# A Soft-MoE macaron kernel on one core: transposes moved from TensorE to VectorE, products packed into row and column groups of the array, loads ordered by use

## The chip, the cores and the metric

The kernel runs on one core of a Trainium2 chip. TensorE (PE) multiplies matrices, its weight loads (PEld) overlap its products, and its results land in PSUM; VectorE (DVE) and ScalarE (ACT) read PSUM, GpSimd (POOL) works on SBUF alone, and SyncE (SP) issues most DMAs. Each engine works through its own queue in order. The metric is the device time of one execution in microseconds. All data is fp32, and each fp32 product of the program appears in the trace as two PE instructions, each with a weight load, while a transpose appears as one.

## The reference

The input `x` has 8 batches of 256 tokens of 128 features. Six blocks are added to it, each on a layernorm of `x`: Soft-MoE (halved), linear attention, Soft-MoE (halved), a ternary GLU (halved), FAVOR+ attention, and the GLU again (halved). Cut to what the change touches:

```python
# Soft-MoE: 16 experts of 64 slots, hidden size 256
x = layernorm(x) * norm_g + norm_b
se = (layernorm(slot_embeds) * slot_g + slot_b) * scale
logits = einsum('bnd,esd->bnes', x, se)
dispatch = softmax(logits, axis=1)               # over the tokens
combine = softmax(logits.reshape(b, n, -1), -1)  # over all 1024 slots
slots = einsum('bnd,bnes->besd', x, dispatch)
gate = gelu(einsum('besd,edf->besf', slots, Wg) + bg)
up = einsum('besd,edf->besf', slots, Wu) + bu
eout = einsum('besf,efo->beso', gate * up, Wd) + bd
out = einsum('bns,bso->bno', combine, eout)

# FAVOR+: 16 heads of 8, 32 random features each
xw = einsum('bhtd,hmd->bhtm', q, proj); xw -= max(xw, -1)
phi = exp(xw) * exp(-0.5 * sum(q * q, -1)) + 1e-6   # for q and for k
KV = einsum('bhtm,bhtd->bhmd', phi_k, v); Ksum = sum(phi_k, over t)
out = einsum('bhtm,bhmd->bhtd', phi_q, KV) / (phi_q . Ksum + 1e-6)
```

## The kernel before

The work is written as small steps: a step names the engines that can do it with a cost on each, the cells that it reads and writes, and a function that issues its instructions. `Plan.place` puts the steps one by one on an engine where they can start first by those costs, and ties are settled by a key; the list `SHIFTS` moves the keys of parts of the program, and its numbers were found by a search. `Plan.issue` then issues every step in the order of its planned start, so the order in each queue is fixed when the program is built. Buffers (`Buf`) come from pools of fixed slots: "comb" (128x2048), "k4" (128x1024), "k2", "k1", "we" (an expert's weights), "ps" (the 8 PSUM banks) and so on.

The 8 batches form two groups of four, the second planned behind the first, so that work of both is mixed. `group` runs, for each of two MoE layers, `dispatch` on its four batches, `experts`, and `combine` with `linear` (linear attention, first layer only); then `glu` on pairs of batches, `favor` on each batch, and `glu` again with the store of `x`.

`dispatch(b)` normalizes a batch (statistics on DVE, L386 and L387; the root on POOL, L392 and L393; the scaling on either, L399), transposes it on PE (L356, the helper of every PE transpose) and forms the logits: 8 products of 128 slots by 256 tokens (L537), copied out to `comb` by L363 (ACT) or L365 (DVE), with a running maximum on DVE (L554). For each half of the slots, DVE takes the maximum over the tokens (L569), ACT the exponentials with their sums (L577), POOL multiplies by the inverse (L590), and since the next product sums over tokens, eight blocks of 128x128 are transposed on PE (L356) and copied out, and L611 gathers the slots with two products of 512 columns. ACT or DVE scales the result into `slots` (L441, L443). For the combine weights, the maximum over the slots is folded (L631), transposed, reduced (L642), spread over the partitions with a product against the identity (L651), subtracted on POOL (L663), and ACT takes the exponential (L669).

`experts` fetches the weights of each of the 16 experts (L688, L689 on SP), forms gate and up for the four batches at once (L703: 256 columns), applies gelu on ACT (L709) and the product on DVE (L714), and forms the down product for two batches at a time (L733: 128 rows that hold two batches' 64 slots), whose bias DVE adds in two instructions on 64 partitions each (L743). `combine` is L772; the hidden layers of `glu` are L990, its other products L1060, L1063 and L1090.

`favor(b)` squares q and k on POOL, sums the squares of each head with products of 16 columns (`half_norms`, L1154), projects q and k with 32-row products in four row groups of the array (`projected`, L1168, with `tile_position`), subtracts the maximum, takes the exponential, adds 1e-6 to phi(k) on POOL (L1200), sums phi(k) with v in products of 33 columns (`sums`, L1230), masks the blocks of the heads (`blocks`), and multiplies with phi(q) in four column groups (`products`, L1261).

Of the kernel before, what the change touches and what calls it, by code (L numbers as in the profile page):

```python
# [16 lines left out]
    -1227, -613, -401, -68, -58, -18, -64, -450, -1382, -1020, -424, -281, -256, -288, -233,  # L17
    -157, -79, -415, -2474, -2414, -2140, -1616, -1392, -1410, -1361, -1647, -1993, -981, -1024,
    -765, -300, -356, -285, -548, -633, -125, 202, -436, 1069, 1221, 47, 271, -1474, 20, 20,
    328, 135, 321, 41, 324, 244, 344, -354, 285, -285, 130, -858, -387, -2, -20, -1081, -1196,  # L20
    -1025, -690, 2, -62, -155, -432, -31, 11, 73, 364, -325, 423, 704, 1277, 1488, 0, -230,
    -498, -161, 261, 336, -1069, -2039, -294, 15, -985, -97, 217, 334, -2546, -904, 699, 282,
    280, 343, -499, -1613, -348, 575, -245, 854, 1080, -1505, 7, 181, -43, 85, 275, 63, 263,
    275, -549, 207, -31, 105, -21, -515, -1151, -524, -514, -318, -600, -516, -298, -150, -63,
    -195, -1899, -1808, -1825, -1479, -1755, -1468, -2181, -1630, -332, -1392, -135, -1924,
    -2484, -1986, -1337, -312, -863, 129, -9, -422, 292, 66, 420, 268, 35, 18, 226, 263, 558,
    1104, 691, -956, -1572, -901, -704, -964, -1303, -1243, -1820, -2476, -2535, -1146, -830,
    -744, 683, -666, -1356, -722, 275, 396, -1669, -293, -1310, -784, 170, 576, 457, 239, 57,
    785, 684, 309, 781, 1213, 1341, 704, 927, 758, 229, 1188, -1400, 467, 1275, -975, 2, 61,
    -923, 156,  # L30
# [34 lines left out]
class Plan:  # L65
# [7 lines left out]
    LAG = {"PE": 300, "ACT": 120, "DVE": 100, "POOL": 150, "SP": 2200}  # L73
# [128 lines left out]
def macaron_kernel(ctx: ExitStack, tc: tile.TileContext, i: dict, out: bass.AP):  # L202
# [27 lines left out]
        "comb": (NJ * N, 9),  # L230
        "slots": (NJ * NB * 4 * S1, G),
        "k4": (1024, 6),
# [3 lines left out]
        "we": (6 * P + D, 3),  # L236
# [5 lines left out]


    for at, cells in (
        (5000, ["begin"]), (7000, [("x", b) for b in range(B)]), (7500, ["small"]),
        (15000, ["weights"]),
    ):
        plan.given(at, cells)
# [11 lines left out]
    def load(name, shape, src=None, eng=nc.sync):  # L260
        t = const.tile(shape, F32, tag=name, name=name)
        eng.dma_start(t, i[name] if src is None else src)
        return t


    x = const.tile([P, NT, D], F32, tag="x", name="x")
    xin = i["L0_attn_x"].rearrange("b (p t) d -> p b t d", t=TT)
    xout = out.rearrange("b (p t) d -> p b t d", t=TT)

    def x_of(b, n=1):  # L270
        return x[:, b * TT : (b + n) * TT, :].rearrange("p (b t) d -> p b t d", t=TT)

    se_raw = Buf("k4", (P, NJ, D))
    sein = i["slot_embeds"].rearrange("(j p) d -> p j d", p=P)
    for h in range(2):
        part = slice(4 * h, 4 * h + 4)
        step(
            {"SP": 100},
            lambda _, part=part: nc.scalar.dma_start(se_raw.ap[:, part], sein[:, part]),
            ["begin"], [(se_raw, h)],  # L280
        )
    nc.sync.dma_start(x_of(0, 2), xin[:, 0:2])
    sg = load("slot_g", [P, 1], eng=nc.scalar)
    sb = load("slot_b", [P, 1], eng=nc.scalar)
    sc = load("scale", [P, 1], i["scale"].partition_broadcast(P), eng=nc.scalar)
    ng = load("norm_g", [P, 1])
    nb = load("norm_b", [P, 1])
    for q in range(1, 4):
        nc.sync.dma_start(x_of(2 * q, 2), xin[:, 2 * q : 2 * q + 2])
    bg = load("bg", [P, E, 2], eng=nc.gpsimd)  # L290
    bu = load("bu", [P, E, 2], eng=nc.gpsimd)
    wqkv = load("WqkvT", [P, 3 * D])
    wproj = load("WprojT", [P, D])
    bproj = load("bproj", [P, D], i["bproj"].partition_broadcast(P))
    w1 = load("w1T", [P, NH])
    w2w = load("w2T", [P, NH])
    s1 = load("s1", [P, NO])
    s2 = load("s2", [P, NO])
    w3s = load("w3T", [P, NO, D], i["w3T"].rearrange("(k p) o -> p k o", p=P))
    s3 = load("s3", [P, D], i["s3"].partition_broadcast(P))  # L300
    wq = load("WqT", [P, D])
    wk = load("WkT", [P, D])
    wv = load("WvT", [P, D])
    wo = load("WoT", [P, D])
    bo = load("bo", [P, D], i["bo"].partition_broadcast(P))
    proj = load("projT", [P, M])
# [5 lines left out]
    def block_mask(n, value, name):  # L312

        w = P // n
        t = const.tile([P, n], F32, tag=name, name=name)
        nc.gpsimd.memset(t, value)
        nc.gpsimd.affine_select(
            out=t, in_=t, compare_op=ALU.is_ge, fill=0.0, base=0,
            pattern=[[-w, n]], channel_multiplier=1,
        )  # L320
        nc.gpsimd.affine_select(
            out=t, in_=t, compare_op=ALU.is_ge, fill=0.0, base=w - 1,
            pattern=[[w, n]], channel_multiplier=-1,
        )
        return t

    m16 = block_mask(H, 1.0, "m16")
    half16 = block_mask(H, 0.5, "half16")
    m4 = block_mask(4, 1.0, "m4")
# [5 lines left out]
    seT = const.tile([P, NJ, 3, S], F32, tag="seT", name="seT")  # L335
# [37 lines left out]
    def normalized(tiles, twice=False):  # L373
# [15 lines left out]
        def root(_):  # L389
            v = mv.ap[:, 1 : 2 * n : 2]  # L390
            eps = EPS * EPS / (1.0 + EPS) if twice else EPS
            nc.gpsimd.tensor_scalar(v, v, eps, None, ALU.add)  # L392
# [3 lines left out]
        step({"POOL": 600 + 160 * n}, root, [mv], [mv])  # L396
        for t, (dst, src, r, w) in enumerate(tiles):
            def apply(e, t=t, dst=dst, src=src):
                (nc.gpsimd if e == "POOL" else nc.vector).tensor_scalar(  # L399
                    dst(), src(), mv.ap[:, 2 * t : 2 * t + 1], mv.ap[:, 2 * t + 1 : 2 * t + 2],  # L400
                    ALU.subtract, ALU.mult,
                )

            step({"POOL": 840, "DVE": 430}, apply, [r, mv], [w])
# [43 lines left out]
    def keys():  # L448
# [8 lines left out]
        for h in range(2):  # L457
            js = range(4 * h, 4 * h + 4)
# [7 lines left out]
            pse = ps_(4, 2, S)  # L466

            def turn(_, pse=pse, js=js):
                for j in js:
                    flip(pse.ap[:, j % 4].rearrange("p k s -> p (k s)"), se_n.ap[:, j, :])  # L470

            step({"PE": flips(4)}, turn, [(se_n, j) for j in js], [pse])
            part = slice(js[0], js[0] + 4)

            def finish(e, pse=pse, part=part):
                if e == "ACT":
                    nc.scalar.activation(
                        seT[:, part, 0:2], pse.ap, AF.Identity, bias=bs, scale=gs
                    )
                else:  # L480
                    nc.vector.tensor_scalar(
                        seT[:, part, 0:2], pse.ap, gs, bs, ALU.mult, ALU.add
# [3 lines left out]
            step({"ACT": act(512, True), "DVE": dve(512, 120)}, finish, [pse, "gs"], cells)  # L486

            def again(_, part=part):
                nc.gpsimd.tensor_copy(seT[:, part, 2], seT[:, part, 0])

            step({"POOL": 400}, again, cells, [("seT2", j) for j in js])

    def weights():

        def block(_):
            nc.vector.tensor_reduce(
# [15 lines left out]
        step({"DVE": 500}, block, ["weights"], ["pbd"])  # L514
        step({"POOL": 1900}, scaled, ["weights"], ["w3s"])

    def dispatch(b, sl):
# [3 lines left out]
        odd, q = b % 2, b % BG  # L527
        y = norm(b, True)
        yt = transposed(y, TT, True)
        comb = Buf("comb", (P, NJ, N))  # L530
        pm = Buf("k2", (P, 2, N))
        for u in range(4):
            pl = ps_(2, N)

            def logits(_, u=u, pl=pl):
                for j in range(2):
                    mm(  # L537
                        pl.ap[:, j, :],
                        seT[:, 2 * u + j, odd : odd + 2].rearrange("p k s -> p (k s)"),
# [841 lines left out]
```

## Time and profile before

| | |
|---|---|
| median of 3 runs | 777.72 us (777.15 to 778.01) |
| the profiled execution | 777.5 us, of which its span is 775.8 us |
| granted clock of TensorE | 0.999 |
| PE, DVE, ACT, POOL busy | 754.0, 528.2, 450.4, 351.2 us |
| PE instructions | 4584 |
| DMA over the span | 36.96 MB, 48 GB/s |
| first PE instruction, first L703, end of the last PE instruction | 11.31, 54.95, about 772 us |

A group of the profile has a line, an engine, an operation, what it writes from what it reads, the shapes and the number of instructions, then its busy time and the mean duration of one in ns, then the idle time of the engine just before it and what ended that. Matmuls are pipelined, so the mean duration of one (276 ns for 128 columns) is longer than what it adds to a row of them. A line of the timeline has start, length and the number of instructions merged in it.

### The profile page before, as it was taken

What the parts mean: (1) busy time and instruction counts of PE and PEld (TensorE: products, weight loads), DVE (VectorE), ACT (ScalarE), POOL (GpSimd) and SP (SyncE); (2) the same over time, 40 slices, a digit from 0 to 9 for tenths busy, and PEclk for the clock granted to TensorE, in tenths of its full rate; (3) what the DMA queues carried; (4) which work ended last, traced back from release to release, by engine and by line L of the source; (5) the groups of instructions that cost most, each with busy time, mean ns of one, the idle gap of its engine ahead of it and who ended that gap; (6) DMA issues with size and microseconds to landing.
All of it is one profiled execution on the core that took longest, in us unless ns stands there. A gap on an engine that the chain in (4) does not pass through costs nothing.

```text
span 775.8 us, 12408 instructions
## 1 busy us (share of the span) xinstructions
PE 754.0 (97%) x4584; PEld 631.6 (81%) x4584; DVE 528.2 (68%) x1156; ACT 450.4 (58%) x824; POOL 351.2 (45%) x376
## 2 busy tenths in 40 slices
PE   2999999999999999999999999999999999999998
PEld 1768787898888988888889879889777887868787
DVE  4899888668988788885645453566865458885422
ACT  1888999555977689987443332345544327543422
POOL 6969454524618356248932123533721326424210
PEclk9999999999999999999999999999999999999999
DMA  7102323203231123232432200000000000000000
GB/s 195 40 0 64 89 65 118 68 29 116 72 114 34 56 68 96 73 86 76 135 95 67 80 1 1 1 1 1 1 1 1 0 15 1 1 1 1 14 0 28
DMA packets 27579, 36.96 MB, mean 48 GB/s; under 512 B 3808, under 2 KB 18816, under 8 KB 27520
## 3 DMA queue, kind: packets, MB, share of 16 engines
q1 hardware_dynamic: 25968, 35.62, 15.6%
q8 instruction: 36, 0.59, 0.3%
q10 hardware_dynamic: 1488, 0.53, 0.3%
q14 instruction: 23, 0.19, 0.1%
q0 software_dynamic: 64, 0.03, 0.0%
HBM read 35.12 MB, written 1.05 MB: 47 GB/s over the span
## 4 chain that ended last, share of the span: by engine, by line
PE 95%; POOL 1%; DVE 1%; DMA 1%; ACT 0%; SPq 0%; issue 0%; POOLq 0%
PE ps L990 25%; PE ps L703 14%; PE ps L772 7%; PE ps L733 7%; PE ps L611 7%; PE ps L537 7%; PE ps L356 6%; PE ps L1090 4%; PE ps L1060 4%; PE ps L1063 4%; PE ps L1230 2%; PE ps L1168 1%; PE ps L1261 1%; PE ps L820 1%; PE ps L651 1%; PE ps L1154 1%
## 5 line engine op out<-in xcount | busy, mean ns | idle before, releaser
L363 ACT COPY k<-ps 128x512 f32<-128x512 f32 (+1 forms) x99 | 51.6, 533 | 128.2 <-PE ps L990 79.7
L703 PE MATMUL ps<-slots,we 128*128 128x256 f32 x512 | 121.0, 380 | 0.0
L703 PEld LDWEIGHTS ps<-slots,we 128*128 128x128 f32 x512 | 93.8, 189 | 16.6 <-issue 4.3
L990 PE MATMUL ps<-comb,comb 128*128 128x256 f32 x448 | 102.8, 380 | 0.0
L990 PE MATMUL ps<-comb,slots 128*128 128x256 f32 x448 | 101.9, 381 | 0.0
L663 POOL TENSOR_TENSOR comb<-comb,k 128x1024 f32<-128x1024 f32 x32 | 75.1, 2365 | 57.3 <-ACT k L577 29.6
L990 PEld LDWEIGHTS ps<-comb,slots 128*128 128x128 f32 x448 | 83.8, 190 | 13.4 <-issue 1.9
L990 PEld LDWEIGHTS ps<-comb,comb 128*128 128x128 f32 x448 | 83.4, 190 | 11.8 <-issue 1.4
L975 POOL TENSOR_TENSOR comb<-comb 128x512 f32<-128x512 f32 x20 | 30.6, 1530 | 123.9 <-ACT comb L1012 73.3
L590 POOL TENSOR_TENSOR k<-k,sm 128x1024 f32<-128x1024 f32 x32 | 60.6, 1903 | 35.7 <-DVE sm L585 34.3
L356 PE MATMUL ps<-ident,k 128*128 128x128 f32 x408 | 60.1, 276 | 15.1 <-POOL k L399 13.6
L714 DVE SCALAR_TENSOR_TENSOR k<-ps,bu,k 128x256 f32<-128x256 f32 x128 | 57.3, 477 | 22.7 <-ACT k L709 21.7
L709 ACT ACTIVATE k<-ps,bg 128x256 f32<-128x256 f32 x128 | 56.4, 473 | 26.1 <-PE ps L703 25.2
L1004 DVE TENSOR_TENSOR comb<-ps,k 128x512 f32<-128x512 f32 x48 | 33.0, 688 | 55.2 <-PE ps L990 31.9
L356 PEld LDWEIGHTS ps<-ident,k 128*128 128x128 f32 x408 | 49.0, 143 | 26.0 <-POOL k L399 14.6
L733 PEld LDWEIGHTS ps<-we,k 128*128 128x128 f32 x512 | 63.9, 192 | 4.9 <-issue 2.4
L743 DVE TENSOR_TENSOR slots<-ps,we 64x256 f32<-64x256 f32 x128 | 53.8, 421 | 20.3 <-PE ps L733 17.4
L537 PE MATMUL ps<-k,seT 128*128 128x256 f32 x256 | 63.4, 389 | 2.5 <-ACT k L441 1.6
L733 PE MATMUL ps<-we,k 128*128 128x128 f32 x512 | 65.4, 275 | 0.0
L577 ACT ACTIVATE k<-comb,sm 128x256 f32<-128x256 f32 x128 | 63.3, 497 | 1.4 <-DVE sm L569 1.2
L1012 ACT ACTIVATE comb<-comb 128x512 f32<-128x512 f32 x48 | 29.9, 628 | 54.2 <-DVE comb L1004 54.1
L772 PE MATMUL ps<-slots,comb 128*128 128x129 f32 x512 | 60.4, 275 | 0.0
(144 smaller groups left out, 1425.5 us busy)
## 6 DMA issues: line engine op xcount, KB each, us to landing
we<-in_We SPq DMA_DIRECT2D x64, 384.0 KB, 3.1
we<-in_bd SPq DMA_DIRECT2D x64, 64.0 KB, 3.1
x<-in_L_attn_x SPq DMA_DIRECT2D x4, 256.0 KB, 5.8
comb<-in_h2T SPq DMA_DIRECT2D x4, 256.0 KB, 3.3
slots<-in_h1T SPq DMA_DIRECT2D x4, 256.0 KB, 4.9
out<-x SPq DMA_DIRECT2D x8, 128.0 KB, 1.7
k<-in_slot_embeds ACTq DMA_DIRECT2D x2, 256.0 KB, 6.2
k<-in_hs SPq DMA_DIRECT2D x2, 256.0 KB, 4.3
```

What stands on the lines that cost most here:

```text
L356: nc.tensor.transpose(po, src, ident)
L537: mm(pl.ap[:, j, :], seT[:, 2 * u + j, odd : odd + 2].rearrange("p k s -> p (k s)"), yt.ap, start=True, stop=True,)
L577: nc.scalar.activation(ex.ap[:, j, :], comb.ap[:, 4 * h + j, :], AF.Exp, bias=mx.ap[:, j : j + 1], accum_out=mx.ap[:, 4 + j : 5 + j],)
L590: nc.gpsimd.tensor_tensor(ex.ap, ex.ap, mx.ap[:, 8:12].unsqueeze(2).to_broadcast([P, 4, N]), ALU.mult)
L611: mm(po.ap.rearrange("p j k s -> p (j k s)"), y.ap[:, t, :], dm.ap[:, t, :], start=(t == 0), stop=(t == TT - 1),)
L663: nc.gpsimd.tensor_tensor(raw, raw, mb.ap.unsqueeze(1).to_broadcast([P, 4, N]), ALU.subtract)
L703: mm(pe.ap[:, m, :], we.ap[:, ts(2 * m + c, P)], sl.ap[:, j, :, k::2, 0:S], start=True, stop=True,)
L709: nc.scalar.activation(ga.ap, pe.ap[:, 0, :], AF.Gelu, bias=bg[:, e, c : c + 1])
L714: nc.vector.scalar_tensor_tensor(ht.ap[:, c, :], pe.ap[:, 1, :], bu[:, e, c : c + 1], ga.ap, ALU.add, ALU.mult,)
L733: mm(po.ap[:, q, :], ht.ap[:, c, ts(q, P)], we.ap[:, ts(4 + c, P)], start=(c == 0), stop=(c == 1),)
L772: mm(po.ap[:, t, 0 : D + 1], comb.ap[:, j, ts(t, P)], eo()[:, j, q, 0 : D + 1], start=(j == 0), stop=(j == NJ - 1),)
L990: mm(bank.ap[:, o], w(k)[:, c, ts(o, P)], rhs().rearrange("p (c n) -> p c n", c=2)[:, c, :], start=(start and o + c == 0), stop=(stop and ...
```

## The change

In the MoE, POOL's divided exponentials are turned by VectorE in place, in blocks of 32x32 (`nc.vector.transpose`), and no longer by PE. The transposed blocks hold tokens in groups of 32 partitions, so the gather is made of 32-row products in four row groups of the array, each with a PSUM bank of its own. Its other operand, the normalized tokens, must then lie four times over the partitions: SP writes them to DRAM in four DMAs and reads them back in four. The exponentials lie in a "comb" buffer. The down products of two experts share the array, 64 columns each, so that the 128 partitions of the result are the two experts' slots and the bias is added in one instruction; the slots have another layout, an expert's front waits for all slots of the four batches, and the biases of two experts are fetched together. The spread of the token maximum is a transpose.

In FAVOR+, the half norms and the sums of phi(k) are formed in four column groups, with the roles of the operands swapped; a copy and PE transposes turn the results back.

The small constants come in one load, the first inputs are loaded in pieces in the order of their use, all on SP; the weights of the later blocks are loaded after that. PE multiplies the identity by itself 14 times at the start, and ACT takes one exponential. Some scalar instructions of POOL have a second operation (times 1.0) or a changed sign. The pools have other numbers of slots, some costs of the planner are changed, and `SHIFTS` has new numbers.

```diff
 kinds:
-        "comb": (NJ * N, 9),
+        "comb": (NJ * N, 10),
-        "k4": (1024, 6),
+        "k4": (1024, 4),
-        "we": (6 * P + D, 3),
+        "we": (6 * P + D, 4),
...
+    plan.key = -100000
+    x_in(0, 1)
+    keys_in(0)
+    fetched(lambda: small, i["small"], [], ["small", "ng"])
+    keys_in(1)
+    x_in(1, 1)
+    keys_in(2)
+    keys_in(3)
+    for b in range(2, B, 2):
+        x_in(b, 2)
+    plan.key = 0
...
 normalized, root:
-            nc.gpsimd.tensor_scalar(v, v, eps, None, ALU.add)
+            m = mv.ap[:, 0 : 2 * n : 2]
+            nc.gpsimd.tensor_scalar(v, v, 1.0, eps, ALU.mult, ALU.add)
+            nc.gpsimd.tensor_scalar(m, m, -1.0, 0.0, ALU.mult, ALU.add)
             nc.gpsimd.tensor_tensor(v, v, power[:, 0:n], ALU.pow)
 normalized, apply:
-                    ALU.subtract, ALU.mult,
+                    ALU.add, ALU.mult,
...
+    def replicated(y, b):
+        yr = Buf("k4", (P, N // 32, D))
+        def spill(_):
+            for k in range(4):
+                nc.sync.dma_start(
+                    spilled[b].rearrange("i (t k) d -> i k t d", k=4)[:, k],
+                    y.ap[32 * k : 32 * k + 32],
+                )
+        def spread(_):
+            for a in range(4):
+                nc.sync.dma_start(yr.ap[32 * a : 32 * a + 32], spilled[b])
+        step({"SP": 1800}, spill, [(y, t) for t in range(TT)], [("y", b)])
+        step({"SP": 1800}, spread, [("y", b)], [yr])
+        return yr
...
 dispatch:
+        yr = replicated(y, b)
...
-            for t in range(TT):
-                pt = ps_(4, P)
-                def turn(_, t=t, pt=pt, ex=ex):
-                    for j in range(4):
-                        flip(pt.ap[:, j, :], ex.ap[:, j, ts(t, P)])
-                step({"PE": flips(4)}, turn, [ex], [pt], takes=[dm])
-                evacuated(
...
-                    mm(
-                        po.ap.rearrange("p j k s -> p (j k s)"), y.ap[:, t, :], dm.ap[:, t, :],
-                        start=(t == 0), stop=(t == TT - 1),
+            def turn(_, part=part):
+                nc.vector.transpose(
+                    ex.ap[:, part].rearrange("p j n -> p (j n)"),
+                    ex.ap[:, part].rearrange("p j n -> p (j n)"),
+                )
+            step({"DVE": 1200}, turn, [(ex, h)], [(ex, h)])
+        pos = [ps_(NJ, 32) for _ in range(4)]
+        def gathered(_):
+            for c in range(N // 32):
+                for a, po in enumerate(pos):
+                    rows = slice(32 * a, 32 * a + 32)
+                    mm(
+                        po.ap, yr.ap[rows, c, :], ex.ap[rows, :, 32 * c : 32 * c + 32],
+                        start=(c == 0), stop=(c == N // 32 - 1), tile_position=(32 * a, 0),
+                    )
+        for a, po in enumerate(pos):
             affinely(
+                lambda a=a: sl.ap[:, :, a // 2, q, 32 * (a % 2) : 32 * (a % 2) + 32],
+                lambda po=po: po.ap, [po], [(sl, "in", q, a)], NJ * 32,
             )
...
 spread:
-                mm(
-                    pb.ap[:, ts(t, P)], mn.ap[:, t : t + 1].to_broadcast([P, P]), ident,
-                    start=True, stop=True,
-                )
+                flip(pb.ap[:, ts(t, P)], mn.ap[:, t : t + 1].to_broadcast([P, P]))
...
 experts, front:
-                    {"PE": mms(256, 256)}, hidden, [we, *whole(j)], [pe], takes=[ga, (ht, c)]
+                    {"PE": mms(256, 256)}, hidden, [we, *whole(j), *filled], [pe], takes=[ga, (ht, c)]
 experts, back:
+                for q in range(BG):
                     for c in range(2):
-                        mm(
-                            po.ap[:, q, :], ht.ap[:, c, ts(q, P)], we.ap[:, ts(4 + c, P)],
-                            start=(c == 0), stop=(c == 1),
-                        )
+                        for k in range(2):
+                            mm(
+                                po.ap[S * k : S * k + S, q, :], hts[k].ap[:, c, ts(q, S)],
+                                wes[k].ap[:, ts(4 + c, P)], start=(c == 0), stop=(c == 1),
+                                tile_position=(0, S * k),
+                            )
...
+                nc.vector.tensor_tensor(
+                    eo()[:, j, :, 0:D], po.ap,
+                    wes[0].ap[:, 6 * P :].unsqueeze(1).to_broadcast([P, BG, D]), ALU.add,
+                )
...
 favor:
-                    mm(
-                        pn.ap[:, k, t, :], qk.ap[:, 1, k, ts(t, P)], half16,
-                        start=True, stop=True,
-                    )
+                    g = 32 * (k * TT + t)
+                    mm(
+                        ph.ap[g : g + 32, :], half32, qk.ap[:, 1, k, ts(t, P)],
+                        start=True, stop=True, tile_position=(0, g),
+                    )
+        evacuated(lambda: hn.ap, lambda: ph.ap, [ph], [hn], P)
+            lambda _: flip(pn.ap.rearrange("p k t h -> p (k t h)"), hn.ap), [hn], [pn],
...
-                    mm(
-                        pk.ap[:, c, :], phi.ap[:, 1, t, ts(c, P)], v1.ap[:, t, c, :],
-                        start=(t == 0), stop=(t == TT - 1),
-                    )
+                        mm(
+                            pk.ap[32 * c : 32 * c + 32, m, :],
+                            ones32 if m else v1.ap[:, t, ts(c, 32)], phi.ap[:, 1, t, ts(c, P)],
+                            start=(t == 0), stop=(t == TT - 1), tile_position=(0, 32 * c),
+                        )
...
+        step({"DVE": 430}, blocks, [pk], [kvm])
+        step({"PE": flips(2)}, turn_sums, [kvm], [pkt])
+        evacuated(
+            lambda: kv.ap, lambda: pkt.ap.rearrange("p a (c n) -> p a c n", c=4), [pkt], [kv], N
+        )
...
+    def rehearse(_):
+        for _ in range(14):
+            mm(pwarm.ap, ident, ident, start=True, stop=True)
```

## The prediction

> **What bounds the kernel now.** I read the busy table first, then the chain of waits, then the table by stretch, to see whether the bound holds everywhere.
>
> ```profile
> PE 754.0 (97%) x4584; PEld 631.6 (81%) x4584; DVE 528.2 (68%) x1156; ACT 450.4 (58%) x824; POOL 351.2 (45%) x376
> PE 95%; POOL 1%; DVE 1%; DMA 1%; ACT 0%; SPq 0%; issue 0%; POOLq 0%
> ```
>
> TensorE is busy for 754.0 of 775.8 us and is 95% of the chain that ended last. The stretches (columns: length, PE, PEld, DVE, ACT, POOL busy, clock, DMA share, GB/s):
>
> ```profile
> 0.00:10.00 10.00, 0.00 (x0) 0.00 (x0) 1.90 (x12) 0.77 (x1) 3.70 (x20) 1.00 0.62 179
> 10.00:20.00 10.00, 5.47 (x13) 3.46 (x14) 7.68 (x38) 2.44 (x4) 9.30 (x15) 1.00 0.79 216
> 20.00:30.00 10.00, 8.35 (x42) 6.91 (x41) 8.53 (x14) 7.04 (x20) 9.72 (x15) 1.00 0.15 57
> 30.00:40.00 10.00, 10.00 (x55) 7.54 (x54) 8.52 (x16) 9.85 (x33) 9.53 (x7) 1.00 0.01 2
> 60.00:70.00 10.00, 10.00 (x57) 7.88 (x56) 9.03 (x22) 9.84 (x16) 9.23 (x5) 1.00 0.16 46
> ```
>
> From 30 us on PE never starves, but until the experts thin out DVE and ACT run at nine tenths too: PE work taken out there counts only as far as they follow. Before 30 us the inputs and then POOL and DVE hold PE back. So the sum is made in PE time, with the opening apart.
>
> Since matmuls overlap, I price an instruction from runs in the timeline: (run − last one's own duration) / (number − 1). An fp32 product is two PE instructions, a transpose one.
>
> ```profile
> 36.05 1.04 PE L356 MATMUL ps<-ident,k 128*128 128x128 f32 x8
> 761.37 1.95 PE L1090 MATMUL ps<-w3T,comb 128*128 128x128 f32 x16
> 525.82 2.54 PE L990 MATMUL ps<-comb,comb 128*128 128x256 f32 x11
> 528.29 1.17 PE L1168 MATMUL ps<-pbd,k 32*128 32x128 f32 x32
> 529.39 1.99 PE L990 MATMUL ps<-comb,comb 128*128 128x256 f32 x8
> 560.77 1.89 PE L990 MATMUL ps<-comb,slots 128*128 128x256 f32 x8
> 562.60 1.07 PE L1261 MATMUL ps<-k,kv 128*32 128x256 f32 x16
> 563.60 1.07 PE L1154 MATMUL ps<-half,k 128*128 128x16 f32 x8
> ```
>
> Transpose (1.04−0.276)/7 = 0.109 us; 128 columns 0.112; 256 columns 0.216 (and 512: 0.429). Sixteen columns (L1154) cost 0.112 as well. L1168 holds four row groups at once: its 32 instructions take 529.39−528.29 = 1.10, eight groups of four at 0.112 plus 0.20; the L990 run ahead takes 2.47 for 11×0.216 = 2.38. So row-grouped work runs at four for one, and entering and leaving it costs 0.20+0.09 = **0.30 us** a block. L1261 (column groups of 32): 1.00 = 4×0.216+0.14, plus 0.10 ahead: **0.23 us** a block.
>
> **What the Trainium skill says.** "TensorE: Matmul & The Clock Gate", Part 3, has four 32-row tiles measured at 3.07 times one; here 32×0.112 = 3.58 us shrinks to 1.10+0.09 = 1.19, 3.0 times, so it agrees. "TensorEngine Tiling (Array Packing)", Key Properties, says that a change of tiling mode drains TensorE, which is the 0.30 and 0.23 us; it lists two tiles of 128×64, which no run shows yet. Part 1 of the first page says that an idle array runs at half clock: the eight L537 instructions at 16.86 take 3.78 us, about 0.43 each against 0.216 later. For the VectorE transpose "VectorE: DVE Perf Modes", The three transpose paths, gives 32×32 blocks and 311 ns for 128x128 bf16; no trace here has one.
>
> **The change, PE time first.**
>
> ```profile
> L356 PE MATMUL ps<-ident,k 128*128 128x128 f32 x408 | 60.1, 276 | 15.1 <-POOL k L399 13.6
> L611 PE MATMUL ps<-k,k 128*128 128x512 f32 x128 | 59.9, 593 | 0.0
> L651 PE MATMUL ps<-ident,sm 128*128 128x128 f32 x64 | 9.7, 276 | 0.0
> L733 PE MATMUL ps<-we,k 128*128 128x128 f32 x512 | 65.4, 275 | 0.0
> L1230 PE MATMUL ps<-kv,comb 128*128 128x33 f32 x128 | 15.0, 273 | 0.0
> L743 DVE TENSOR_TENSOR slots<-ps,we 64x256 f32<-64x256 f32 x128 | 53.8, 421 | 20.3 <-PE ps L733 17.4
> L569 DVE TENSOR_REDUCE sm<-comb 128x4 f32<-128x1024 f32 x32 | 38.6, 1209 | 0.1
> ```
>
> 1. Dispatch, 16 times. Out: 16 transposes (16×0.109 = 1.74) and eight L611 instructions (8×0.429 = 3.43). In: 32 products of 256 columns in four row groups, 64 instructions in 16 groups of four: 16×0.216+0.30 = 3.76. 1.41 less, **−22.6 us**.
> 2. Token maximum spread by transposing: 64×0.112 → 32×0.109, **−3.7**.
> 3. Expert down products: 512×0.112 = 57.3 becomes 1024 instructions on 64-column halves. If pairs run side by side, 512×0.112 again, plus 32 blocks×0.23: **+7.4**. Bounds: below, no switch cost, 0; above, no overlap, +57.3. I take +7.4, since both group shapes that the trace shows overlap fully.
> 4. FAVOR+, 8 times. Half norms: 8×0.112 → two groups of four, a switch and a transpose, 0.22+0.23+0.11: −0.34. Sums: 16×0.112 → 8×0.112+0.23+2×0.109: −0.45. Together **−6.3**. The new waits (norms → copy → transpose; sums → mask → transpose → copy) stand in PE's queue mostly with other matmuls between, often eight L990 (1.7 us), against 0.4 us copies; what queues behind PE is everything, so I keep +2 for them in the range.
>
> Sum −25.2 us. PE's start-to-start work is 775.8−11.3 (first matmul)−3.7 (after the last) = 760.8. All instructions at the prices above come to 744; the other 16 are gaps, 9 of them before 30 us and 7 later (switches, short stalls). 744 becomes 719.
>
> **The other engines.** DVE: L743's 128×0.42 = 53.8 become 32 of 128x512, at the 0.69 of such PSUM reads (L1004) 22: −32. In come 32 transposes of 128x1024. Bounds: an instruction of 128x1024 [...] as in L569, 1.2 us; twice that if fp32 goes at half rate: +38 to +77. I take 1.2. Copies of the PE transposes (64 of 128x512, by the copies counted in both built programs about 31 fewer on ACT and 33 on DVE) go: −22 and −18; slot copies get smaller and twice as many: ACT +9. DVE ends near 521, ACT near 440, of 755: enough cover on average. Buffers: the exponentials take a "comb" slot now; with both groups' four results held, two of the ten are free for them, so two dispatches at a time can be under way, as few as DVE can feed.
> POOL: half constants and sign changes make two-operand forms; one instruction more per norm (48×0.23 = 11). What the new forms take is not shown: for L1200 between 1.1 (a 512-wide L1132) and the 2.8 measured, for L399 0.48 (DVE's) to 0.82. I count 0: POOL has 55% to spare after the opening.
> SP: eight issues more a dispatch (y to DRAM, four row copies back), 128×0.43 = 55 us of a queue that mostly waits. From y, the copies need 8×0.43 and two landings of about 3 us, 9.5 us. Meanwhile y is transposed, logits (3.5), maximum (1.2), exponentials (2), division (1.9) and transposes (1.2) pass on the other branch: over 10 us, so hidden, with 1 us to spare at worst; if a "we" load ahead of it in SP waits, that margin goes and L644, with all of PE behind it, waits.
> Loads by use: x of batch 0 (128 KB) is alone in front; its first statistic waited for it to 7.96, now to about 4.2 (0.8 issue, 3 to land, as small loads do). All opening loads now go through SP, ten issues at 0.45 to 5.3 us, and leave ACT's queue and POOL's (bg and bu, 1.35 us). The 14 practice products (28×0.21 = 6 us cold) run on an idle PE and save the 1.7 us of half clock, but they may hold the first transposes to about 9.5.
>
> **The opening.** The first expert product (L703) came at 54.95. In the order of the built program all four gathers and their slot copies stand ahead of it now. PE needs by then only 32×0.109+64×0.216+4×3.76 = 32.4 us. DVE has ahead of the last slot copy, each at its duration less the 0.08 us by which neighbours overlap (L554 and L365 start at 25.09, 25.69 and 26.29 and last 0.68): 22 statistics at 0.40, 12 maxima at 0.60, 8 reductions and 8 transposes at 1.12, 16 norms and affines at 0.45, 7 folds and copies at 0.5, 15 small at 0.13: 46 us. Before, DVE was busy 86% of the time from its first data to 54.95; 46/0.88 from 4 us on gives **56 us**. So the faster loads are spent on the transposes, and the opening, not PE, sets that date.
> Span = 56 + (719−32.4) + 7 (gaps later, as before: 16 less the 9 before 30 us) + 3.7 = **753**; 2 us for FAVOR's waits and SP: 755. The profiled execution took 777.5 for a span of 775.8, and the median is 777.72: **757 us**.
>
> **Rivals.**
> A. Openings shrink as the loads do: DVE starts 4 us earlier and POOL's norms halve, first expert at 46: 10 less, 747. For: POOL at 9.3 to 9.7 of 10 there. Against: DVE's 46 us. 0.12.
> B. DVE becomes the bound of the MoE: transposes of 2.4 us put 9.6 us on the opening, and in stretches like 60:70 DVE has one tenth left: 767 to 772. 0.12.
> C. (slower) The two 64-column halves take turns: 57.3 on top, 757+57−7 = **807**. For: no run shows the shape, and twice the weight loads come with it. Against: L1168 and L1261. It decides from 0.152 us a pair (0.112 + the 20.7 us left / 512). 0.07.
> D. (slower or nothing) Late copies through DRAM: PE waits at every gather. From 1.3 us each (16×1.3 = 20.7) the gain is gone; at 2 us it is 757+32 = 789. For: SP's fetches wait up to 45.5 us for a "we" buffer (its waits), and copies queue behind them. Against: the 10 us branch. 0.06, with it that the order searched anew doesn't fill PE, at the same price.
> The forecast as worked: 0.63, with its own range 749 to 766.
>
> **Numbers.** Faster (over 0.2%, 1.6 us, about what runs from 777.15 to 778.01 can tell): 0.63+0.12+0.12 less 0.02 = 0.85; within 0.2%: 0.03; slower: 0.12. Range 744 to 772: the forecast, A and B.
>
> **What would show it.** Right: L644 as 1024 instructions in about 60 us; L356's line down to 272 transposes; L768 near 65 us; DVE transposes at 1.1 to 1.3 us; first expert product at 50 to 60; PE full after that at a busy total near 730. Wrong: L768 over 78 us (C); idle of PE before L644 with a DMA or SP named (D); PE gaps beyond 60 us ended by DVE (B).

## The result, and the profile after

The changed kernel takes **781.44 us** (median of 5 runs, 779.5 to 782.22), the kernel before 777.65 us (5 runs, 777.15 to 778.01). The ratio is 1.0044 with a 95% interval of 1.0027 to 1.0061: slower by 0.4%, where 757 us were forecast (744 to 772). The profiled execution took 779.5 us for a span of 777.8. The page of after, its busy table, its chain, and the groups that answer to those of before:

```profile
PE 745.5 (96%) x5884; PEld 625.3 (80%) x5884; DVE 523.8 (67%) x1085; ACT 436.1 (56%) x806; POOL 319.9 (41%) x418
...
PE 91%; DVE 3%; DMA 2%; POOL 1%; SPq 1%; issue 1%; ACT 0%; ACTq 0%; POOLq 0%
...
L737 PE MATMUL ps<-slots,we 128*128 128x256 f32 x512 | 123.6, 392 | 16.5 <-DMA we<-in_We 16.5
...
L644 PE MATMUL ps<-comb,k 32*128 32x256 f32 x1024 | 66.2, 399 | 3.2 <-issue 1.3
...
L768 PE MATMUL ps<-we,k 128*64 128x128 f32 x1024 | 62.5, 276 | 0.0
```

L737 is the old L703, the gate and up products of the experts, whose line before was:

```profile
L703 PE MATMUL ps<-slots,we 128*128 128x256 f32 x512 | 121.0, 380 | 0.0
```

Its idle time is new: 16.5 us, ended by the weight loads, where before PE never waited for an expert's weights. L644, the new gather, waits only 3.2 us, and no DMA is named as the end of it. The chain has 91% of PE where it had 95%, and DMA and SP's queue 3% together. The stretches of after (the columns are those of the table before):

```profile
10.00:20.00 10.00, 7.88 (x31) 6.13 (x32) 7.63 (x22) 5.49 (x13) 7.09 (x19) 0.83 0.54 162
...
30.00:40.00 10.00, 10.00 (x74) 7.79 (x75) 8.05 (x13) 8.05 (x25) 5.66 (x4) 0.70 0.94 261
60.00:70.00 10.00, 10.00 (x49) 8.78 (x49) 8.94 (x17) 8.84 (x12) 7.49 (x11) 1.00 0.38 94
200.00:220.00 20.00, 14.83 (x165) 12.61 (x163) 14.12 (x31) 10.02 (x22) 5.87 (x14) 0.92 0.35 96
220.00:240.00 20.00, 17.48 (x118) 14.66 (x119) 10.99 (x19) 12.18 (x28) 11.31 (x7) 0.82 0.44 144
```

PE starts earlier (7.88 of 10 us busy from 10 to 20, where it had 5.47), runs at a clock of 0.70 from 30 to 40, and is full at 60, as it was before. The loss lies further back: between 200 and 240 PE has holes, and its clock is low in the same stretches. Before, these two had neither:

```profile
200.00:220.00 20.00, 20.00 (x119) 16.75 (x118) 17.99 (x36) 18.84 (x43) 12.49 (x12) 1.00 0.32 93
220.00:240.00 20.00, 20.00 (x115) 16.63 (x115) 16.13 (x33) 15.79 (x35) 7.23 (x6) 1.00 0.39 114
```

One of the holes, in PE's timeline of after:

```profile
207.69 1.97 PE L768 MATMUL ps<-we,k 128*64 128x128 f32 x32
209.59 3.72 PE L737 MATMUL ps<-slots,we 128*128 128x256 f32 x16
...
214.23 0.60 PE L359 MATMUL ps<-ident,k 128*128 128x128 f32 x4
222.52 2.05 PE L737 MATMUL ps<-slots,we 128*128 128x256 f32 x4 [7.69 <-DMA we<-in_We]
```

And SP's timeline at the same place (a line with a count joins neighbours that follow each other):

```profile
210.12 5.68 SPq L532 DMA_DIRECT2D y<-k  x8
215.97 2.78 SPq L539 DMA_DIRECT2D k<-y  x6
218.79 0.90 SPq L717 DMA_DIRECT2D we<-in_We  x2
```

The down product that ends at 209.6 frees two "we" buffers. The next weights are issued at 218.79 only: SP's queue holds eight copies of y to DRAM first, which cannot start before y is there (210.12), then their way back. The issues alone take 8.5 us, the weights 3.7 us more to land, and PE stands still for 7.69. The three holes are at 78.7, 214.8 and 322.2 us (3.7, 7.7 and 5.1 us).

Where the time went, in PE's time from the start of one instruction to that of the next: each kind of instruction at its usual distance (row- and column-grouped ones at what a full group costs) sums to 744.3 us before and 704.5 after, 3.1 of them practice products. What is left is gaps, half clock and switches:

| | before | after | e5_sp_manual (below) |
|---|---|---|---|
| up to 60 us | 9.5 | 24.2 | 25.0 |
| 78 to 90, 212 to 235, 318 to 335 us | 1.4 | 23.0 | 4.3 |
| elsewhere (switches of tiling mode, short waits) | 5.4 | 21.2 | 21.0 |

So 39.8 us of PE's work did go, and PE's first instruction, now a practice product, comes 9.7 us earlier (1.57 for 11.31). Against that stand 14.7 us more in the opening, 15.8 in the last row, and 21.6 in the three stretches, which turn the gain into a loss. By the same sum, instructions in row- or column-grouped blocks and just ahead of them hold 15.6 us of the last row after and 4.2 before, so 11.4 of the 15.8 are the new switches.

### The profile page after: what moved, and what is told of

It reads as the page before. It is cut to its first block, busy times and chain, and to the rows that moved or that the text cites. A ratio compares the mean times of both kernels' runs of the same rounds, so it can differ in the third digit from the quotient of the medians.

```text
span 777.8 us, 15141 instructions
## 1 busy us (share of the span) xinstructions
PE 745.5 (96%) x5884; PEld 625.3 (80%) x5884; DVE 523.8 (67%) x1085; ACT 436.1 (56%) x806; POOL 319.9 (41%) x418
## 4 chain that ended last, share of the span: by engine, by line
PE 91%; DVE 3%; DMA 2%; POOL 1%; SPq 1%; issue 1%; ACT 0%; ACTq 0%; POOLq 0%
PE ps L1027 25%; PE ps L737 15%; PE ps L768 8%; PE ps L809 7%; PE ps L644 7%; PE ps L568 6%; PE ps L359 4%; PE ps L1127 4%; PE ps L1100 4%; PE ps L1097 4%; DMA we<-in_We 1%; PE ps L1206 1%; PE ps L1272 1%; PE ps L1306 1%; PE ps L857 1%; DVE sm L602 1%
## 5 line engine op out<-in xcount | busy, mean ns | idle before, releaser
L737 PE MATMUL ps<-slots,we 128*128 128x256 f32 x512 | 123.6, 392 | 16.5 <-DMA we<-in_We 16.5
L737 PEld LDWEIGHTS ps<-slots,we 128*128 128x128 f32 x512 | 97.6, 197 | 32.0 <-issue 19.4
L743 ACT ACTIVATE k<-ps,small 128x256 f32<-128x256 f32 x128 | 57.3, 474 | 61.4 <-PE ps L737 59.6
L623 POOL TENSOR_TENSOR comb<-comb,sm 128x1024 f32<-128x1024 f32 x32 | 60.8, 1905 | 64.8 <-DVE sm L618 64.6
L748 DVE SCALAR_TENSOR_TENSOR k<-ps,small,k 128x256 f32<-128x256 f32 x128 | 57.2, 476 | 38.4 <-ACT k L743 37.9
L366 ACT COPY k<-ps 128x512 f32<-128x512 f32 (+2 forms) x67 | 33.5, 503 | 87.9 <-PE ps L1027 61.9
L644 PE MATMUL ps<-comb,k 32*128 32x256 f32 x1024 | 66.2, 399 | 3.2 <-issue 1.3
L610 ACT ACTIVATE comb<-comb,sm 128x256 f32<-128x256 f32 x128 | 63.2, 497 | 6.8 <-DVE sm L602 6.8
L644 PEld LDWEIGHTS ps<-comb,k 32*128 32x128 f32 x1024 | 56.3, 196 | 9.9 <-issue 3.0
L768 PEld LDWEIGHTS ps<-we,k 128*64 128x64 f32 x1024 | 55.3, 137 | 9.4 <-issue 4.3
L768 PE MATMUL ps<-we,k 128*64 128x128 f32 x1024 | 62.5, 276 | 0.0
L809 PEld LDWEIGHTS ps<-slots,comb 128*128 128x128 f32 x512 | 58.6, 192 | 1.3 <-issue 1.2
```

Of the source, the lines that this page charges most:

```text
L366: nc.scalar.copy(dst(), src())
L610: nc.scalar.activation(ex.ap[:, 4 * h + j, :], comb.ap[:, 4 * h + j, :], AF.Exp, bias=mx.ap[:, j : j + 1], accum_out=mx.ap[:, 4 + j : 5 + j],)
L623: nc.gpsimd.tensor_tensor(ex.ap[:, part], ex.ap[:, part], mx.ap[:, 8:12].unsqueeze(2).to_broadcast([P, 4, N]), ALU.mult,)
L644: mm(po.ap, yr.ap[rows, c, :], ex.ap[rows, :, 32 * c : 32 * c + 32], start=(c == 0), stop=(c == N // 32 - 1), tile_position=(32 * a, 0),)
L737: mm(pe.ap[:, m, :], we.ap[:, ts(2 * m + c, P)], sl.ap[:, j, k, :, 0:S], start=True, stop=True,)
L743: nc.scalar.activation(ga.ap, pe.ap[:, 0, :], AF.Gelu, bias=bg[:, e, c : c + 1])
```

## The experiments

The cause to test, **theory Q**: the y copies hold back the expert weights in SP's queue. The list of engines whose order is fixed by the plan has no SP in it, in either kernel:

```python
engines = {nc.tensor.engine, nc.scalar.engine, nc.vector.engine, nc.gpsimd.engine}
with tc.manual_schedule(engines=engines):
    plan.issue(home)
```

SP's queue is thus ordered by the framework, without the plan's dates.

**e5_sp_manual.** SP joins the list:

```diff
-    engines = {nc.tensor.engine, nc.scalar.engine, nc.vector.engine, nc.gpsimd.engine}
+    engines = {nc.tensor.engine, nc.scalar.engine, nc.vector.engine, nc.gpsimd.engine, nc.sync.engine}
```

> As after, but SP too issues in the order of the plan (in both kernels SP's queue is ordered by the framework's own scheduler, only PE, ACT, DVE and POOL follow the plan). If the late weights come from that order: the waits for 'we' fall by half or more and the time to 765 to 772 us. If they come from the copies' length as such (4.2 us of issue and a landing per dispatch, against 3.6 in the plan), the waits stay near 16 us and the time at 775 to 782 us. Rival O: 777 to 782 us.

761.2 us (760.36 to 763.21), ratio to before 0.9789 (0.977 to 0.9808): 20 us less by one line. SP's timeline at the place shown above, and PE's wait for weights in the whole run (us in total, times, longest):

```profile
204.85 4.78 SPq L717 DMA_DIRECT2D we<-in_We  x3
...
210.95 5.78 SPq L532 DMA_DIRECT2D y<-k  x8
216.90 3.71 SPq L539 DMA_DIRECT2D k<-y  x8
```

```profile
PE ps L737 <- DMA we<-in_We: 1.1, 1, 1.1
```

The copies are issued at nearly the same date and take as long; but the weights now go ahead of them, as soon as the buffers are free. The three stretches fall from 23.0 to 4.3 us, by 18.7; the two spans, 777.8 and 759.7, differ by 18.1.

**c1_before_sp.** The same line in the kernel before.

> The kernel before, with the one line of e5_sp_manual: SyncE's queue is issued in the planned order as well. Theory Q (the order of SP's queue matters only where the y copies stand in it; before has none, and its PE never waited for an expert's weights): 777.6 us, between 775.5 and 779.5, no PE wait of L703 on "we". Rival S (SP in the planned order is a gain of its own, whatever the change): about 761 of 781 as in e5, that is 757 to 765 us.

781.71 us (780.99 to 782.08), ratio 1.005 (1.0037 to 1.0063). The planned order of SP is no gain of its own: without y copies it is 4 us worse. The first L703 comes at 56.73 instead of 54.95, and two waits for weights of 1.9 us together appear. I had expected no difference (775.5 to 779.5), so this is a miss; why the framework's order is the better one there was not tried.

**e1_merged_sp.** One DMA out and one back, on SP, in place of four and four:

```diff
-            for k in range(4):
-                nc.sync.dma_start(spilled[b].rearrange("i (t k) d -> i k t d", k=4)[:, k], y.ap[32 * k : 32 * k + 32])
+            nc.sync.dma_start(spilled[b].rearrange("i (t k) d -> k i t d", k=4), y.ap)
...
-            for a in range(4):
-                nc.sync.dma_start(yr.ap[32 * a : 32 * a + 32], spilled[b])
+            nc.sync.dma_start(yr.ap, spilled[b].unsqueeze(0).to_broadcast([4, 32, N // 32, D]))
```

> The y copies of a dispatch are one DMA to DRAM and one back (a source repeated over four row groups) in place of four and four, still on SP; all else as after. Theory Q (expert weights are late because SP's one queue issues the y copies ahead of them: 16.5 us of PE waits for 'we', some 23 us with the half clock that follows): SP's copies shrink from 4.2 us of issue per dispatch to about 1, the three waits of PE for 'we' shrink by half or more, 10 to 18 us faster than after, 763 to 771 us. Rival O (the opening and VectorE's transposes hold PE back, the waits for 'we' would be replaced by others): 777 to 782 us, as after.

832.55 us (831.77 to 835.14), ratio 1.071 (1.0683 to 1.0736): far slower, a miss. The waits of PE and of SP:

```profile
PE ps L736 <- DMA we<-in_We: 63.4, 5, 22.8
```

```profile
SPq L536 <- DMA y<-k: 61.7, 16, 12.3
```

There are fewer issues, but SP now stands 3.9 us on average, 12.3 at worst, for the copy to reach DRAM before it can issue the way back, and the weights stand behind that. The time that a merged copy costs SP is mostly this wait, not its issues. The copies themselves are slower too: with only merged copies under way the 16 DMA engines are a quarter busy, while in after, with four and four under way, they are nearly three quarters busy and move twice as much (e1 first, then after; the last two columns are DMA share and GB/s):

```profile
78.00:81.00 3.00, 1.68 (x32) 1.44 (x28) 2.79 (x7) 3.00 (x10) 3.00 (x2) 1.00 0.25 101
```

```profile
68.60:72.40 3.80, 3.80 (x43) 3.26 (x41) 3.80 (x6) 3.75 (x7) 0.00 (x0) 1.00 0.73 200
```

The sign was wrong; that a blocked SP makes the weights late is shown all the more.

**e2_merged_pool.** The same merged copies, issued by POOL.

> The same two merged y copies, issued from GpSimd's queue, so that none stands ahead of the expert weights on SP. Theory Q: PE's waits for 'we' go nearly all, 20 to 25 us faster than after, 755 to 761 us, if GpSimd, 41% busy, does not suffer from waiting for y; each copy that blocks it for 2 us costs at most 32 us of its slack. Rival O: 777 to 782 us.

799.33 us (798.8 to 800.8), ratio 1.0278. PE waits 18.7 us for weights, in three places. The issues by queue (KB each, median us to landing), and the landing of the weights:

```profile
k<-y POOLq DMA_DIRECT2D x16, 512.0 KB, 11.8
y<-k POOLq DMA_DIRECT2D x16, 128.0 KB, 5.6
```

```profile
DMA to landing us min/median/max: 2.4/3.8/14.8
```

Out and back take 17.4 us where each of four and four takes 1.9 and 2.7 from its issue to its landing. Some weights, issued on a queue with no copies in it, now land as late as 14.8 us. That they share the DMA engines with the long copies would explain it (the 16 engines are 0.97 busy from 85 to 90 us, with such weights under way), but was not tried by itself. As a test of Q the run is spoiled by that, and the four and four copies on another queue than SP's were not tried.

**e4_no_turns.** The 32 transposes by VectorE are left out (the gather then multiplies unturned exponentials):

```diff
             def turn(_, part=part):
-                nc.vector.transpose(
-                    ex.ap[:, part].rearrange("p j n -> p (j n)"),
-                    ex.ap[:, part].rearrange("p j n -> p (j n)"),
-                )
+                pass
```

> As after, without the 32 VectorE transposes of 128x1024 (the exponentials go to the gather unturned; 39 us of VectorE work and their place in the chain from exponential to gather are gone). Rival O, VectorE bound: first expert product about 8 us earlier than 60.0, and PE gaps elsewhere fall too, 10 us or more faster than after, 765 to 770 us. Theory Q: the waits for 'we' stay, only the opening gains a few us, 775 to 779 us.

781.75 us (781.11 to 784.81), ratio 1.0058 (1.0039 to 1.0078), with VectorE 493.1 us busy instead of 523.8. PE still waits 16.0 us for weights. So VectorE's load does not set the time while the weights come late; the same was not tried on e5, where they don't. Nor does it alone set the opening: the gathers end at 56.7 instead of 58.7, but the first expert product comes at 60.10, since transposes of the second group's tokens stand ahead of it in PE's queue and wait for POOL:

```profile
49.57 7.25 PE L641 MATMUL ps<-comb,k 32*128 32x256 f32 x124 [0.22 <-ACT slots L446]
...
59.50 0.76 PE L359 MATMUL ps<-ident,k 128*128 128x128 f32 x2 [1.22 <-POOL k L404]
60.10 1.90 PE L734 MATMUL ps<-slots,we 128*128 128x256 f32 x8
```

**c2_favor.** The kernel before with the FAVOR+ part and the spread by transposes alone:

```diff
-                        pn.ap[:, k, t, :], qk.ap[:, 1, k, ts(t, P)], half16,
+                        ph.ap[g : g + 32, 0, :], half32, qk.ap[:, 1, k, ts(t, P)],
...
+                            ones32 if m else v1.ap[:, t, ts(c, 32)], phi.ap[:, 1, t, ts(c, P)],
...
-                    pb.ap[:, ts(t, P)], mn.ap[:, t : t + 1].to_broadcast([P, P]), ident,
+                flip(pb.ap[:, ts(t, P)], mn.ap[:, t : t + 1].to_broadcast([P, P]))
-        "k2": (512, 7),
-        "k1": (256, 14),
+        "k2": (512, 8),
+        "k1": (256, 13),
```

> The kernel before, with two parts of the change alone: the half norms and the sums of phi(k) in four column groups, and the token maximum spread by a transpose (two banks are shared where the change takes two each, one more k2 buffer and one k1 fewer, so that the plan finds room). No copy, transpose by VectorE or pair of experts is in it. If steps 2 and 4 of the prediction were sized rightly (-3.7 and -6.3 us of PE): 767.6 us, up to 2 more for FAVOR's new waits; PE busy total 10 to 12 us below 754.0. Rival W (the new waits in FAVOR+ eat what the fewer columns save): 773 to 780 us, with idle of PE ahead of the L1206-like products named after a copy of ACT or DVE.

808.23 us (807.74 to 808.9), ratio 1.0396 (1.0382 to 1.041). PE's work by the sum above falls from 744.3 to 730.9, switches apart, as it should; but gaps grow from 16.3 to 59.7 us, spread over the whole run. 808 lies outside both ranges that were expected. `SHIFTS` was searched for other steps and pools; that its order is bad for these is likely, but was not tried. The run confirms the work that goes and cannot price the new waits: here a part of the change could not be tried alone without a new search.

**o1_warm** and **o2_short**, both on e5. The first gathers run at half clock, after gaps of PE. o1 fills two places with practice products, o2 takes those at the start away:

```diff
 o1_warm, in the first dispatch only
         def gathered(_):
+            if early:
+                for _ in range(12):
+                    mm(pos[0].ap.rearrange("p j s -> p (j s)")[:, 0:P], ident, ident, start=True, stop=True)
...
         def spread(_):
+            if early:
+                for _ in range(10):
+                    mm(pb.ap[:, 0:P], ident, ident, start=True, stop=True)
 o2_short
         def rehearse(_):
-            for _ in range(14):
+            for _ in range(1):
```

> e5_sp_manual with 12 practice products of the identity (2.7 us at full clock) at the head of the first gather, and 10 (2.2 us) ahead of the first spread of the token maximum, so that PE is not idle in the two places after which the first and the second gather ran at half clock (7.9 and 5.8 us for 64 and 68 instructions, against 3.7 us later). Theory H (this lost clock is on the path of the opening, and is what makes the first expert product come at 60 and not at the predicted 56): the first gather takes 3.7 to 4.5 us, the first L737 comes 4 to 5 us earlier (56 to 57.5 instead of 61.2), and the run takes 756 to 758 us. Rival V (VectorE and GpSimd bound the opening, 46 and 43 of its 60 us): the gathers shorten, the first L737 stays within 1.5 us of 61.2, 760 to 763 us.

> e5_sp_manual with 1 practice product at the start instead of 14. The prediction said that the 14 save 1.7 us of half clock, and may hold the first transposes to 9.5. If that is so: 1.7 us later, 763 us. Rival V (VectorE and GpSimd bound the opening): the same time as e5, 761.2 within 1 us, as PE's early work is not what the first gather waits for. A third outcome, earlier by up to 1 us, if the transposes had waited for the practice.

o1: 760.81 us (760.46 to 762.33), 0.9787 (0.9773 to 0.98). The first gather shortens from 7.9 to 5.2 us with its start later, so that it ends only 0.7 us earlier, and the first expert product comes at 61.06 instead of 61.19; the spread that I had filled turned out not to stand in the second gap, and the second gather kept its 5.84 us. The edit was badly aimed and says little. o2: 761.79 us (760.68 to 762.7), 0.9795 (0.9781 to 0.9808), the same as e5: the 14 practice products at the start gain nothing that can be measured.

**f1_order, f2_order, f3_order_sp_free.** e5 with `SHIFTS` searched again against measured durations (f1 and f2, two results of 202 numbers each; f1's begin with 1731, -8790, -2498, -1835), and f1 with SP outside the plan again (f3).

```diff
 f3_order_sp_free, against f1_order
-    engines = {nc.tensor.engine, nc.scalar.engine, nc.vector.engine, nc.gpsimd.engine, nc.sync.engine}
+    engines = {nc.tensor.engine, nc.scalar.engine, nc.vector.engine, nc.gpsimd.engine}
```

> e5_sp_manual with other numbers in SHIFTS, searched on the planner's own placing with the steps then given the durations that the traces of after and e5 show (a gather 3.95 us with its mode switch, a spill of y 2.7, a pair's down product 2.04). On that model the order of e5 takes 756.2 us (its measured span was 759.7), the new one 752.6. Theory L (what is left above 757 is the order of the opening and short waits): 757.5 us, between 755 and 760, and the first L737 a microsecond or two earlier than 61.2. Rival B (the model's 3.6 us are less than what it gets wrong, half clock after gaps above all): 760 to 764 us, no gain on e5.

> As f1_order, from another start of the search: 753.0 us on the same model, its first expert product 2 us later than f1's by the model (60.8 against 58.8). If the date of the first expert product sets the end (the sum of the prediction: span = that date + PE's work), f2 takes 2 us longer than f1. If it does not, since PE's other work fills the time before it as well, f2 takes 756 to 759 like f1.

> f1_order with SyncE's queue again outside the planned order, as in the changed kernel. Theory Q (the loss is made in SP's queue, where the y copies stand ahead of the experts' weights): the order of the other engines does not mend it, 772 to 785 us, with PE waits of L737 on "we" of 10 us and more. Rival R (the changed kernel's order was merely a poor one): within 3 us of f1.

f1 761.34 us (758.58 to 761.9), ratio 0.9778 (0.976 to 0.9796): no gain on e5. f2 759.39 (758.93 to 759.86), 0.9761 (0.9748 to 0.9775). f3 777.42 (772.97 to 778.52), 0.9989 (0.9978 to 1.0), and its wait:

```profile
PE ps L739 <- DMA we<-in_We: 11.2, 3, 4.7
```

| median us | SP ordered by the framework | SP in the plan |
|---|---|---|
| kernel before | 777.7 | 781.7 |
| changed kernel, its order | 781.4 | 761.2 |
| changed kernel, order f1 | 777.4 | 761.3 |

With the y copies, SP's order decides 16 to 20 us in both orders of the other engines that were tried; without them it decides 4, the other way. In f2 the first expert product came at 57.53 and not after f1's 61.24, as the search's model had it; the median was 2 us shorter. The date may count, at about half; the two orders differ elsewhere too.

**g_warm2.** f2 with 14 practice products in the one gap ahead of its first gather:

```diff
+        early = len(done) == 2
+        done.append(b)
...
         def spread(_):
+            if early:
+                for _ in range(14):
+                    mm(pb.ap[:, 0:P], ident, ident, start=True, stop=True)
```

> f2_order with 14 practice products of the identity (3.0 us at full clock) in the one gap of PE ahead of its first gather (33.2 to 36.4 us, ended by the token maximum), after which that gather took 7.02 us for 68 instructions at a clock of 0.50, against 4.15 for 66 in the next. From 36.4 us on PE has no gap in f2 until the first expert product at 57.53. Theory H (half clock after a gap is a cost of the opening, and here it lies on the path): the first gather takes 3.9 to 4.3 us, the first expert product comes at 54.5 to 55.5, and the run takes 756.5 us, between 755.5 and 757.5. Rival V (the gathers behind it wait for VectorE's transposes and copies anyway): new gaps ahead of the second or third gather, first expert within 1 us of 57.5, 758.5 to 760 us.

757.92 us (755.76 to 761.45), ratio 0.9753 (0.9731 to 0.9774). PE's timelines of f2 (first line) and of g:

```profile
36.96 7.02 PE L646 MATMUL ps<-comb,k 32*128 32x256 f32 x68
```

```profile
33.04 3.29 PE L688 MATMUL ps<-ident 128*128 128x128 f32 x28
...
36.65 4.91 PE L647 MATMUL ps<-comb,k 32*128 32x256 f32 x68
43.23 0.69 PE L647 MATMUL ps<-comb,k 32*128 32x256 f32 x2 [1.67 <-DVE slots L450]
...
56.52 3.69 PE L746 MATMUL ps<-slots,we 128*128 128x256 f32 x16
```

The first gather loses 2.1 of its 7.02 us, the next one waits 1.67 for a slot copy, and the first expert product gains 1.0. For that date both theories are half right: half clock was on the path to it, and a wait for VectorE came next. Against f2 the gain cannot be told from nothing (the intervals overlap). It is the fastest median of all, 2.5% under before.

## Why the prediction was wrong, and where it was right

**PE's work (steps 1 to 4) was right.** The sum forecast, 719 us, holds 15.8 us of new switches (16×0.30 + 32×0.23 + 8×0.46), so about 703 without them; the trace has 704.5−3.1 = 701.4. A gather at full clock takes 3.72 us a block of 64 (forecast 3.76 with its switch). A pair's down product takes 1.90 us from its start at 207.69 to the next (forecast 2.02): the two column halves do overlap, as taken in step 3, and rival C is false. The switches show in the last row of the table, with 11.4 us more than before outside the opening and the three stretches.

**The other engines were right, except POOL.** VectorE 523.8 (forecast 521), ScalarE 436.1 (440). The changes that the prediction lists for VectorE add up to 513 to 517, not 521, so part of this nearness is luck. The transpose, bounded between 1.2 and 2.4 us, takes 1.23, which speaks against rival B. POOL, counted as no change, fell from 351.2 to 319.9; what that was worth in time was not tried. Three groups of after:

```profile
L631 DVE STREAM_TRANSPOSE comb<-comb 128x1024 f32<-128x1024 f32 x32 | 39.4, 1233 | 1.5 <-POOL comb L623 0.6 <-POOL slots L788 0.6
...
L404 POOL TENSOR_SCALAR k<-x,sm 128x128 f32<-128x128 f32 x59 | 27.4, 470 | 3.4
...
L1238 POOL TENSOR_SCALAR comb<-comb 128x1024 f32<-128x1024 f32 x8 | 8.6, 1079 | 53.9 <-ACT comb L1233 53.6
```

**The SP step failed.** I priced the 128 new issues at 55 us "of a queue that mostly waits", and asked only whether the copies would be late for the gather, behind a waiting "we" load. What they do to the loads behind them was put at nothing, without a reason. The gather was never the victim. It was the other way round: copies ahead of the loads. A queue that mostly waits is the dangerous one, for its waits and issues are in order, and whatever comes behind inherits them. Rival D named SP's queue as the place and late copies as the mechanism, and is false as stated; the right one, weights behind copies, was nobody's. The kernel's description above takes SP's order for the plan's. It was read off `Plan.issue` without the list of engines around it. The issue was also underpriced: eight spills take 5.68 us at the place shown, 0.71 each, not 0.43 (the median of all 64 issues is 0.59), while the reads back are near it (2.78 for 6). Cost: the three stretches, 21.6 us over before, of which the bare waits are 16.5 and the half clock after two of them most of the rest.

**The opening was 4 us off.** The first expert product came at 60.01, not 56, and not at rival A's 46. Part of this is arithmetic: the terms listed for VectorE add up to 46.6, and at the 86% that the prediction reads they give 58, where it divides 46 by 0.88. VectorE's "46 us" was not the bound by itself either (e4). Two things stand in its place: the first two gathers ran at half clock (7.6 and 5.8 us against 3.7, so 6 us, not all of it on the path, by g), and the second group's transposes stood ahead of the first expert (e4). How much each is worth is open.

**The sum.** Forecast span 755; plus 4 for the opening and some 19 for the weights (18.7 by e5) is 778, against 777.8 measured; this sum was made afterwards, from the measured terms. With SP's order mended, the kernel as changed takes 761.2, inside the range and 4 over the forecast.

## What to carry to other kernels

When a change puts new DMAs into a queue, list what will stand behind each of them and when that is needed, with the wait of the DMA counted as well as its issue; a low-use queue is no shelter. Find out who orders each queue: a plan that knows the copies' cost is of no use for an engine that does not follow it. And when a large gain in the bound engine's work shows up as nothing, sum its instructions at their usual distance first: that says whether the work is still there or the time has turned into gaps, and the gaps name their releaser.

## What the hardware showed that I had not expected

- **A gap can cost more than itself.** In e5 the clock is 1.00 from 20 to 30 us, PE is idle for most of 27.8 to 30.8, and from 31 to 37 it is 0.50. In after PE goes on at half clock for 4.6 us behind the hole of 7.7 us and for 5.6 behind that of 5.1; behind the one of 3.7 us the clock stays at 1.00. The Trainium skill, "TensorE: Matmul & The Clock Gate", Part 1, has the clock fall after an idle window of about 3.4 us and rise after a busy one; the traces agree in kind, with a half clock in e5 of about two such windows. The granted clock over the span was 0.980 in after, 0.989 in e5, 0.993 in f2 and 0.998 in g.
- **The merged DMAs were not cheaper than four small ones.** Issued by POOL (e2), 128 KB out in one landed in 5.6 us against 1.9 for each of four on SP, and 512 KB back in one in 11.8 against 2.7; there the issuing engine had changed as well. On SP (e1) merged copies kept the DMA engines a quarter busy, at 101 GB/s against 200 with four and four.
- **The form of POOL's scalar operations matters.** With a multiplication by 1.0 beside the addition, 128x1024 took 1.08 us instead of 2.79 (L1238, before L1200), and 1.05 in c2, which changes little else on POOL. 128x128 with the sign changed (addition, not subtraction; L404, before L399) took a median of 0.45 us instead of 0.81 on POOL; on VectorE the same change left it at 0.35.
